# One hand-planned instruction list for four layers instead of three lists, and a new order of the first transfers

## The chip, the cores and the metric

One core of a Trainium2 chip runs the whole program. The metric is device time in microseconds of one execution, as the median of several runs. The engines are PE (TensorE, matrix products), DVE (VectorE), ACT (ScalarE), POOL (GpSimd) and SP (SyncE, which here issues every DMA). Each engine works through its own queue strictly in order; they meet at semaphores.

## The reference

Four layers run one after another on four images of 192 channels and 56 x 56 pixels, all in float32:

```
# layer 0: batch norm over the batch, 1x1 conv to q, k, v (6 heads of 32)
xn   = (x - mean) * rsqrt(var + eps) * gamma + beta        # mean, var over all four images
attn = softmax(conv7x7([q * scale, k]) + rel_bias)          # 49 logits per head and pixel
out  = sum over the 49 neighbours of attn * v               # then projection, residual
x    = x1 + c2(gelu(c1(x1)))                                # MLP of 768
# layer 1: a gate for each channel
filt = chosen per channel from 32 cosine bases, by a small network on image 0
y    = relu(bn1(w1d @ sum(pooled7x7(x) * filt)))            # one number per image and channel
x    = x * y + x
# layer 2: attention in overlapping 8x8 windows (stride 6), folded back by adding
out  = fold(exp(q k + bias - max) v) / fold(sum)            # projection, then gate by
out  = sigmoid(dwconv3(3x - pools of 2, 4, 8)) * out        # local high frequencies
x1   = x + out
x    = x1 + fc2(z1 * dwconv3(layer_norm(z2)))               # z1, z2 = gelu(fc1(norm(x1)))
# layer 3: selective scan in four directions
u    = silu(dwconv3(in_proj(norm(x)))); z = silu(...)
h_t  = exp(dt_t * A) * h_(t-1) + dt_t * B_t * u_t;  y_t = C_t h_t   # 4 states a channel
x    = x + out_proj(norm(sum of four directions) * z)
```

## The kernel before

**Staging.** `layers01` does layers 0 and 1, `layer2` and `layer3` the others. Between them whole images stand in DRAM (`x1`, `x2`). Channels lie on 96 partitions in two halves; pixels are cut into chunks of 448 (8 rows of an image, 7 chunks in each). Each of the three functions opens its own memory pools, loads its packed weights (`load_packs`, L219), clears and prepares its tiles, and closes its pools at the end, so the next function's tiles lie where the last one's were and can be written only when those are done.

**The order of the instructions.** Inside each function the work is written as many generators (threads), and a planner, the class `Order`, puts their steps into one list at build time. A step is yielded as an engine, a modelled cost, the buffers it takes and, for ACT, a table of functions. The planner keeps a model time for each engine. At every step it looks at the first 130 threads by their `place`, works out when each could start, and takes the one with the smallest start + 0.05 x place. Thus place is a soft priority in units of 0.05 us, and the queue of each of PE, ACT, DVE and POOL is this list, fixed at build time and run in order. There are three planners, one for each function, each beginning with model time zero and an empty list. The statements ahead of the planner's run (loads, clears, constants) are not in the list.

**The start.** `layers01` issues on SP: the three weight packs, 24 fills of `vmem` borders with zeros (L383, L385), then the four images (L391), each into a buffer from which DVE takes `bn_stats` (L394). The first image stays in `x`; the others share two buffers, so the fourth transfer waits until the statistics of the second are done. From the statistics come `bn_a`, `bn_c` (L402 to L404); PE multiplies them with weights (L421, L434); POOL clears `qk_in`, `xc` and `lg` (L482); then ACT copies the first pixels (L519) and PE makes values (L529, stored to `vmem` at L552) and the 7x7 convolution (L634).

**From layer 1 to layer 2.** DVE's `aggregate` steps (L789, L794, L803) end layer 0's attention. `mlp` then runs on PE and ACT for the last chunks (L869, L878, L884); `gate` (L1014 to L1042) forms one scale for each channel, loads each chunk back from `mid` (L1048), scales it on ACT (L1051, two instructions for each of 7 chunks) and stores it (L1053). Three buffers `xc` serve this. `layer2` then loads weights, multiplies weights with biases (L1111, L1124, L1136), clears 14 groups of tiles on POOL (L1158), and its first band `front(0)` loads rows (L1237), normalises them (L1193 to L1215), clears borders on POOL (L1242, L1251) and multiplies them to q and k (L1262).

**From layer 2 to layer 3.** Layer 2 is a chain of bands: `front`, `quad` (windows), `back`, then for each chunk `head`, `grow` and `tail` with two depthwise convolutions on DVE (nine taps each, L1341 and L1343) and products on PE up to L1506. After the last quad only heads, grows and tails are left. `layer3` loads weights, clears tiles on DVE and POOL (L1727, L1737, L1739) and starts with `begin(b, c)` for each chunk: a norm (L1768 to L1789), a product, and a depthwise convolution into `u`, for image 0 on DVE (L1855, L1857) and for the others on PE. From them come `prod` in DRAM, from which `load`, `sizes`, `decay` and `scan` run (L1989 to L2131); a scan group is one step of 448 pixels for half the channels, 56 groups for each image.

Of the kernel before, what the change touches and what calls it, by code (L numbers as in the profile page):

```python
# [20 lines left out]
HW = H * W  # L21
HALF = 96
# [218 lines left out]
class Order:  # L241
# [12 lines left out]
    def __init__(self, nc, **kinds):  # L254
        self.nc = nc
        self.engines = {}
        self.kinds = {k: [[0.0, t] for t in tiles] for k, tiles in kinds.items()}
        self.threads = []
        self.table = None
        self.end = 0.0  # L260

# [10 lines left out]
    def add(self, place, gen):  # L272
        self.threads.append([place, len(self.threads), gen, 0.0, next(gen)])

    def start(self, th):
# [10 lines left out]
        for kind in set(takes):  # L286
            n = takes.count(kind)
            free = sorted(s[0] for s in self.kinds[kind] if s[0] is not None)
            if len(free) < n:
                return None  # L290
            t = max(t, free[n - 1])
# [4 lines left out]
    def run(self):  # L296
        self.threads.sort(key=lambda th: th[:2])
        while self.threads:
# [7 lines left out]
            for th in over:  # L306
                self.threads.remove(th)
# [12 lines left out]
            if th[4] is None:  # L320
                self.threads.remove(th)
# [26 lines left out]

EXP_LN, GELU = "natural_log_exp_and_others", "gelu_and_others"
# [3 lines left out]
def layers01(tc, x_in, packs, aps, dst):  # L353
# [6 lines left out]
    with ExitStack() as ctx:  # L360
        const = ctx.enter_context(tc.tile_pool(name="a_const", bufs=1))
        dram = ctx.enter_context(tc.tile_pool(name="a_dram", bufs=1, space=DRAM))
        w = load_packs(nc, const, packs, aps)
        ident = const.tile([128, 128], F32, name="a_ident")
        make_identity(nc, ident)


        NG = HEADS // 2
        vmem = [dram.tile([NG, PADW, PADW, 64], F32, name=f"vmem{j}") for j in range(2)]
        x = const.tile([128, 2, HW], F32, name="x")  # L370
        nc.gpsimd.memset(x[HALF:], 0.0)
        mid = [dram.tile([C, HW], F32, name=f"mid{b}") for b in range(B)]


        bn_a = const.tile([HALF, 2], F32, name="bn_a")
        bn_c = const.tile([HALF, 2], F32, name="bn_c")
        with tc.tile_pool(name="a_stat", bufs=2) as sp:
            zero = sp.tile([PADW, 3 * 64], F32, name="zero", bufs=1)
            nc.vector.memset(zero, 0.0)
            for v in vmem:  # L380
                for g in range(NG):
                    for y in (0, PADW - 3):
                        nc.sync.dma_start(v[g][:, y : y + 3].rearrange("x y c -> x (y c)"), zero)  # L383
                    for y in (0, PADW - 3):
                        nc.sync.dma_start(  # L385
                            v[g][y : y + 3].rearrange("x y c -> y x c"), zero.rearrange("p (x c) -> p x c", c=64)
                        )
            stats = sp.tile([HALF, 2, B * NCHUNK, nc.vector.BN_STATS_DIM], F32, name="stats", bufs=1)
            for b in range(B):
                t = x[:HALF] if b == 0 else sp.tile([HALF, 2, HW], F32, name="xs")  # L390
                nc.sync.dma_start(t, pixels(x_in[b]))  # L391
                for h in range(2):
                    for c in range(NCHUNK):
                        nc.vector.bn_stats(stats[:, h, b * NCHUNK + c, :], t[:, h, c * CH : (c + 1) * CH])  # L394
            mv = sp.tile([HALF, 2, 2], F32, name="mv", bufs=1)
            for h in range(2):
                nc.vector.bn_aggr(mv[:, h, :], stats[:, h].rearrange("p a b -> p (a b)"))
            std = sp.tile([HALF, 2], F32, name="std", bufs=1)
            nc.vector.tensor_scalar_add(std, mv[:, :, 1], EPS)
            nc.scalar.activation(std, std, AF.Sqrt)  # L400
            nc.vector.reciprocal(std, std)
            nc.vector.tensor_mul(bn_a, w["a96.bn_gamma"], std)  # L402
            nc.vector.tensor_mul(bn_c, mv[:, :, 0], bn_a)
            nc.vector.tensor_sub(bn_c, w["a96.bn_beta"], bn_c)  # L404


        qk_scale = const.tile([128, 1], F32, name="qk_scale")
        nc.vector.memset(qk_scale, 1.0)
        for r in range(2):
            nc.vector.memset(qk_scale[64 * r : 64 * r + 32, :], HD**-0.5)  # L410
        qk_bias = const.tile([128, HEADS], F32, name="qk_bias")
        v_bias = const.tile([112, C], F32, name="v_bias")
        rel_bias = const.tile([128, HEADS], F32, name="rel_bias")
        nc.sync.dma_start(v_bias, aps["vb"].to_broadcast([112, C]))
        nc.vector.tensor_scalar_add(rel_bias, w["a128.rel"], w["a128.dm_b"])
        with tc.tile_pool(name="a_ps0", bufs=1, space=PSUM) as ps0, tc.tile_pool(name="a_sb0", bufs=1) as sb0:
            pq = ps0.tile([128, HEADS], F32, name="pq")
            for r in range(2):
                for hd in range(HEADS):
# [1779 lines left out]
```

## Time and profile before

| what | value |
|---|---|
| median of 3 runs | 6847.67 us (6843.52 to 6848.31) |
| profiled execution, its own time | 6850.6 us |
| its span | 6848.8 us |
| DVE busy | 5982.6 us, 87%, 7513 instructions |
| PE busy | 5770.1 us, 84%, 43558 instructions |
| ACT busy | 2621.1 us, 38%, 4063 instructions |
| POOL busy | 1409.3 us, 21%, 1401 instructions |
| layers 0 and 1 | about 0 to 2992 us |
| layer 2 | about 2992 to 4909 us |
| layer 3 | about 4909 to 6849 us |

Times inside the program are counted from the span's start. An engine's share over the whole span is a mean over stages with different limits, so the views to read are those of single stretches: where both busy engines are low together, no engine sets the pace but a chain of waits. The chain view follows the work that ended last backwards, and shows in order of time what each piece was and how long it took. A tile's name stands left of the arrow, its sources right of it.

### The profile page before, as it was taken

How to read it: one execution, taken by the hardware profiler on the slowest of the kernel's cores; microseconds unless marked ns; L12 is line 12 of the kernel's file. 1: busy time of each engine (PE TensorE's matmuls, PEld its weight loads, DVE VectorE, ACT ScalarE, POOL GpSimd, SP SyncE). 2: the span in 40 equal slices, each digit the busy share in tenths (PEclk: the TensorE clock that was granted, in tenths of full speed). 3: DMA queues.
4: the chain of work that ended last, by engine and by line, in shares of the span. 5: the costliest groups of instructions: out<-in, count | busy, mean ns of one | idle time of the engine just before them, and what ended most of it. 6: DMA issues, size and time to landing. Idle time of an engine off the chain costs nothing.

```text
span 6848.8 us, 107270 instructions
## 1 busy us (share of the span) xinstructions
PE 5770.1 (84%) x43558; PEld 2650.3 (39%) x43558; DVE 5982.6 (87%) x7513; ACT 2621.1 (38%) x4063; POOL 1409.3 (21%) x1401
## 2 busy tenths in 40 slices
PE   4999979999999996768888788886579889889777
PEld 2445434444444442335444444453223223222211
DVE  2799999999999999828999899898687887887997
ACT  1111112222222111125555455454266666666544
POOL 0000000000000000022122322220114544544564
PEclk9999989999999998879999899997799999999998
DMA  3222112221222113120000000000035565655654
GB/s 95 57 53 64 36 29 57 55 66 36 51 62 66 36 38 80 45 58 16 18 16 17 17 19 15 19 18 9 24 99 131 145 157 128 161 135 137 170 150 117
DMA packets 252042, 462.65 MB, mean 68 GB/s; under 512 B 30388, under 2 KB 237964, under 8 KB 240412
## 3 DMA queue, kind: packets, MB, share of 16 engines
q1 hardware_dynamic: 251548, 455.80, 26.4%
q8 instruction: 343, 5.62, 0.4%
q14 instruction: 151, 1.24, 0.1%
HBM read 238.58 MB, written 62.96 MB: 44 GB/s over the span
## 4 chain that ended last, share of the span: by engine, by line
DVE 49%; PE 35%; issue 7%; ACT 5%; DMA 2%; POOL 2%; SPq 0%; DVEq 0%; POOLq 0%; ACTq 0%
DVE pr L789 9%; DVE oa L794 7%; PE a_bank L634 6%; DVE bg L1343 5%; DVE ob L794 4%; PE c_bank L1864 4%; DVE st L2103 3%; DVE bxn L1343 3%; PE c_bank L1821 2%; PE a_bank L869 2%; PE a_bank L884 2%; PE c_bank L2081 2%; PE c_bank L2126 2%; DVE c_bank L2087 2%; PE bank L1506 1%
## 5 line engine op out<-in xcount | busy, mean ns | idle before, releaser
L789 DVE TENSOR_TENSOR pr<-vdx,attn 112x1792 f32<-112x1792 f32 (+4 forms) x720 | 1185.6, 1648 | 19.0
L634 PE MATMUL a_bank<-qk_in,w_a 64*49 64x392 f32 x9408 | 1161.2, 497 | 0.0
L2110 POOL TENSOR_TENSOR da<-st,bc 128x448 f32<-128x448 f32 x672 | 856.6, 1280 | 840.1 <-DVE st L2103 632.1
L794 DVE TENSOR_TENSOR oa<-oa,pr 112x1792 f32<-112x1792 f32 (+1 forms) x423 | 764.9, 1808 | 0.0
L634 PE MATMUL a_bank<-qk_in,wd 64*49 64x392 f32 x4032 | 694.6, 496 | 0.0
L2103 DVE TENSOR_TENSOR_SCAN st<-da,st,c_bank 128x448 f32<-128x448 f32 x576 | 647.2, 1133 | 0.7 <-ACT da L2056 0.7
masks.py:197 POOL MEMSET b_ident<- 128x128 f32 x1 | 0.2, 205 | 2857.5 <-DVE sc L1042 2857.5
L634 PEld LDWEIGHTS a_bank<-qk_in,w_a 64*49 64x49 f32 x9408 | 432.4, 120 | 397.7 <-issue 392.9
L2087 DVE TENSOR_TENSOR c_bank<-c_bank,bc 128x448 f32<-128x448 f32 x672 | 382.6, 617 | 113.1 <-PE c_bank L2081 112.6
L315 ACT ACT_TABLE_LOAD x372 | 477.3, 1283 | 6.5
L2056 ACT ACTIVATE da<-da,a_neg 128x448 f32<-128x448 f32 x672 | 413.8, 658 | 114.7 <-DMA da<-dt 112.8
L1343 DVE SCALAR_TENSOR_TENSOR bg<-bzpad,w_b,bg 128x448 f32<-128x448 f32 (+2 forms) x672 | 424.1, 687 | 0.0
L2126 PE MATMUL c_bank<-da,w_c 128*32 128x448 f32 x1344 | 352.2, 570 | 72.1 <-POOL da L2110 65.5
L794 DVE TENSOR_TENSOR ob<-ob,pr 112x1792 f32<-112x1792 f32 (+3 forms) x282 | 393.1, 1394 | 0.0
L878 ACT ACTIVATE hm<-a_bank,w_a 128x448 f32<-128x448 f32 x168 | 106.2, 633 | 641.7 <-PE a_bank L869 619.3
L869 PE MATMUL a_bank<-xc,w_a 128*128 128x448 f32 x672 | 297.4, 572 | 64.1 <-DVE xc L854 64.1
L2081 PE MATMUL c_bank<-du,w_c 32*128 32x448 f32 x1344 | 260.6, 624 | 105.8 <-DVE du L2071 62.9
L634 PEld LDWEIGHTS a_bank<-qk_in,wd 64*49 64x49 f32 x4032 | 249.2, 120 | 256.6 <-issue 254.7
L1432 PE MATMUL bank<-bxn,w_b 128*128 128x448 f32 (+2 forms) x672 | 293.6, 566 | 23.7 <-DVE bxn L1215 17.8
L586 ACT ACTIVATE qk_in<-a_bank,qk_bias,qk_scale 64x224 f32<-64x224 f32 (+5 forms) x288 | 146.1, 525 | 420.8 <-PE a_bank L571 418.5
L884 PE MATMUL a_bank<-hm,w_a 128*96 128x448 f32 x672 | 288.5, 561 | 21.1 <-ACT hm L878 21.0
L1864 PE MATMUL c_bank<-pad,diag 128*96 128x448 f32 (+2 forms) x756 | 297.4, 543 | 2.3 <-ACT pad L1832 2.3
(307 smaller groups left out, 9937.9 us busy)
## 6 DMA issues: line engine op xcount, KB each, us to landing
da<-dt SPq DMA_DIRECT2D x672, 224.0 KB
vdx<-vmem SPq DMA_DIRECT2D x168, 476.0 KB
bc<-prod SPq DMA_DIRECT2D x224, 224.0 KB
row<-x SPq DMA_DIRECT2D x56, 336.0 KB
x<-x SPq DMA_DIRECT2D x4, 2352.0 KB
vmem<-vt SPq DMA_DIRECT2D x56, 168.0 KB
xc<-x SPq DMA_DIRECT2D x56, 168.0 KB
mid<-xc SPq DMA_DIRECT2D x56, 168.0 KB
```

The lines of the kernel that those rows point to most:

```text
L315: self.nc.scalar.preload_act_table_set(table)
L634: nc.tensor.matmul(py[a][outs[g], : 7 * W].rearrange("p (y x) -> p y x", x=W), wt[halves[a], dx], q[halves[a], r, i0 + m : i0 + m + 7, dx ...
L789: nc.vector.tensor_mul(pr, vv, wt)
L794: nc.vector.tensor_add(og, og, before)
L869: nc.tensor.matmul(ph[:, :CH], w["a128.c1T"][:, k, 128 * m : 128 * m + 128], xt[:, k], start=(k == 0), stop=(k == 1),)
L884: nc.tensor.matmul(acc[h][:HALF, :CH], w["a128.c2T"][:, m, HALF * h : HALF * h + HALF], hm, start=(m == 0), stop=(m == 5),)
L1343: nc.vector.scalar_tensor_tensor(dst, x, wt[:, t : t + 1], dst, ALU.mult, ALU.add)
L1864: nc.tensor.matmul(rows2(pc[:HALF, : n * W]), diag[:, h, t], pad[:, h, at + t // 3 : at + t // 3 + n, t % 3 : t % 3 + W], start=(t == 0), ...
L2087: nc.vector.tensor_mul(tiles[j][:, :SCH], tiles[j][:, :SCH], b_)
L2103: nc.vector.tensor_tensor_scan(sts[j][:, r], da[:, r], tiles[j][:, :SCH][:, r], first, ALU.mult, ALU.add)
L2110: nc.gpsimd.tensor_mul(da, sts[j], c_)
L2126: nc.tensor.matmul(py[32 * j : 32 * j + 32, :SCH], w["c128.sum"], das[j], start=True, stop=True)
```

## The change

1. **One list.** There is one `Order` for all functions. Threads can be added while it runs (`add` with a layer's name, sorted in by place), kinds of buffers can be given later (`give`), and it counts the open threads of each layer. `layer2` and `layer3` become generators that are themselves threads of the list, at places 84 and 240. Their loads, clears and constants become steps. Layer 2's threads get 150 added to their places, layer 3's 330.
2. **Memory from two sides.** What layer 0's attention alone uses (`x`, `qk_in`, `vdx`, `pr`, `attn` and others) lies on the right side, the rest of layers 0 and 1 on the left. When the last sums are done, the right side is closed and layer 2's weights and most of its tiles are put there and cleared. When all threads of layers 0 and 1 have been placed, their left side is closed and layer 2's tiles for windows are put there; `bxn` is now cleared on DVE. When all quads and bands are placed, that left side goes to layer 3's weights, rows and `u` of image 0, and its threads join the list; `begin` of image b asks that layer 2's tails of that image are placed. When layer 2 has no open thread, `y`, the second `u` and the buffers of the scans take the right side.
3. **The start.** The images are issued first, then the weights, `v_bias`, and the zero fills.
4. **The last image's gate.** For image 3 the scaling runs on POOL as `tensor_scalar_mul`; the other images stay on ACT.

The diff without its changes of indentation, cut:

```diff
 class Order:
...
+    def give(self, **kinds):
+        for k, tiles in kinds.items():
+            self.kinds[k] = [[self.end, t] for t in tiles]
...
-    def add(self, place, gen):
-        self.threads.append([place, len(self.threads), gen, 0.0, next(gen)])
+    def add(self, place, gen, layer):
+        self.open[layer] += 1
+        bisect.insort(self.threads, [place, next(self.count), gen, self.end, next(gen), layer])
+
+    def drop(self, th):
+        self.threads.remove(th)
+        self.open[th[5]] -= 1
...
+BASE2, BASE3 = 150, 330
...
-def layers01(tc, x_in, packs, aps, dst):
+def layers01(tc, pools, x_in, packs, aps, dst):
...
+    ctx, early, dram, banks = pools["01"], pools["01 sums"], pools["dram"], pools["banks"]
+    att = early.enter_context(tc.tile_pool(name="a_att", bufs=1, side="right"))
-        w = load_packs(nc, const, packs, aps)
...
-        x = const.tile([128, 2, HW], F32, name="x")
+    x = att.tile([128, 2, HW], F32, name="x")
...
+        stats = sp.tile([HALF, 2, B * NCHUNK, nc.vector.BN_STATS_DIM], F32, name="stats", bufs=1)
+        for b in range(B):
+            t = x[:HALF] if b == 0 else sp.tile([HALF, 2, HW], F32, name="xs")
+            nc.sync.dma_start(t, pixels(x_in[b]))
...
+        w = load_packs(nc, const, packs, aps)
+        nc.sync.dma_start(v_bias, aps["vb"].to_broadcast([112, C]))
             for v in vmem:
                 for g in range(NG):
...
-            stats = sp.tile([HALF, 2, B * NCHUNK, nc.vector.BN_STATS_DIM], F32, name="stats", bufs=1)
...
+        if u == NG * B - 1:
+            order.marks.add("sums of 01")
...
-                yield on_act(CH, CH, ready=order.end + 3)
                 for h in range(2):
+                if b < B - 1:
+                    yield on_act(CH, ready=None if h else order.end + 3)
                     nc.scalar.activation(xt[:HALF, h], xt[:HALF, h], AF.Copy, scale=sc[:, h : h + 1])
+                else:
+                    yield on_pool(CH, each=0.0015)
+                    nc.gpsimd.tensor_scalar_mul(xt[:HALF, h], xt[:HALF, h], sc[:, h : h + 1])
...
-def layer2(tc, src, packs, aps, dst):
+def layer2(tc, order, pools, src, packs, aps, dst):
...
+    yield lambda: "sums of 01" in order.marks
+    pools["01 sums"].close()
+    const = ctx.enter_context(tc.tile_pool(name="b_const", bufs=1, side="right"))
+    yield on_sp()
     w = load_packs(nc, const, packs, aps)
+    there = order.end + 12
...
+    for t in (*xl, *sq, *xn2s, p, apad, *zpads):
+        yield on_pool(1500)
+        nc.gpsimd.memset(t, 0.0)
...
+    yield on_pe(8 * 80, "bank", ready=there)
...
+    yield lambda: order.open["01"] == 0
+    pools["01"].close()
...
+    for i in range(2):
+        yield on_dve(1700)
+        nc.vector.memset(xns[i], 0.0)
+        for t in (qs[i], ks[i]):
+            yield on_pool(1600, each=0.0009)
+            nc.gpsimd.memset(t, 0.0)
+    for t in accs:
+        yield on_pool(3400, each=0.0009)
+        nc.gpsimd.memset(t, 0.0)
+    order.give(xl=xl, sq=sq)
...
-def layer3(tc, src, packs, aps, dst):
+def layer3(tc, order, pools, src, packs, aps, dst):
...
+    yield lambda: "2" in order.marks and order.at2["quad"] == 100 and order.at2["back"] == 20
+    pools["2 quads"].close()
+    const = pools["3"].enter_context(tc.tile_pool(name="c_const", bufs=1))
+    yield on_sp()
     w = load_packs(nc, const, packs, aps)
+    there = order.end + 8
...
+    for t in (*rows, *sqs, *pads):
+        yield on_dve(900)
+        nc.vector.memset(t[HALF:], 0.0)
+    yield on_pool(6000)
+    nc.gpsimd.memset(us[0][HALF:], 0.0)
...
         def begin(b, c):
...
+        yield lambda: order.at2["tail"] >= NCHUNK * (b + 1)
...
+    yield lambda: order.open["2"] == 0
+    pools["2"].close()
+    late = pools["3"].enter_context(tc.tile_pool(name="c_late", bufs=1, side="right"))
...
+    us += [late.tile([128, 2, HW], F32, name="u1")]
+    y = late.tile([128, 2, HW], F32, name="y")
...
-            layers01(tc, [x[b] for b in range(B)], packs[0], aps[0], x1)
-            layer2(tc, x1, packs[1], aps[1], x2)
-            layer3(tc, x2, packs[2], aps[2], [out[b] for b in range(B)])
+            order = layers01(tc, pools, [x[b] for b in range(B)], packs[0], aps[0], x1)
+            order.add(84, layer2(tc, order, pools, x1, packs[1], aps[1], x2), "later")
+            order.add(240, layer3(tc, order, pools, x2, packs[2], aps[2], [out[b] for b in range(B)]), "later")
+            with tc.manual_schedule(engines=engines):
+                order.run()
```

## The prediction

> **What bounds the kernel now.** I read the page first, then the busy times of stretches around the three places that the change touches, then the chain of waits there. The page gives the span, the busy time of each engine, and the busy tenths of 40 slices of 171.2 us each.
>
> ```profile
> span 6848.8 us, 107270 instructions
> ...
> PE   4999979999999996768888788886579889889777
> ...
> DVE  2799999999999999828999899898687887887997
> ...
> PEclk9999989999999998879999899997799999999998
> ```
>
> Inside the layers DVE or PE stands at 9 or near it; both are low together in slice 1 (start), slice 18 (2911 to 3082 us, layer 1 ends, layer 2 begins: PE 6, DVE 2) and slice 29 (4794 to 4965, layer 2 ends, layer 3 begins: 5 and 6). DVE is busy 5982.6 us of 6848.8, so 866 us hold all of its idle time. The next view gives busy time of each engine in the stretches of those places (columns: length, then busy time and count of PE, PEld, DVE, ACT, POOL, then clock, DMA share, GB/s).
>
> ```profile
> 0.00:94.00 94.00, 0.00 (x0) 0.00 (x0) 38.30 (x82) 1.89 (x4) 6.03 (x7) 1.00 0.60 154
> ...
> 2966.00:3025.60 59.60, 14.35 (x52) 10.08 (x52) 5.34 (x16) 10.76 (x18) 33.48 (x24) 0.50 0.39 116
> 4790.00:4909.00 119.00, 70.44 (x136) 29.51 (x136) 80.96 (x129) 33.35 (x40) 3.72 (x7) 0.73 0.03 8
> 4909.00:4999.00 90.00, 52.33 (x118) 20.31 (x119) 60.63 (x82) 32.35 (x43) 22.48 (x19) 0.77 0.20 57
> ```
>
> PE does nothing for 94 us; no engine but POOL is half busy in the second stretch; DVE is idle 38 us of the third and 29 of the fourth. The chain of waits (start, length, what) names what ends each hole:
>
> ```profile
> 38.63 23.77 DMA xs<-x
> 62.42 7.48 DVE stats L394 x14
> 69.92 14.11 DMA xs<-x
> ...
> 2989.16 2.77 DMA x<-xc
> 2992.15 3.02 POOL bxn L1158 x2
> ...
> 3024.94 0.63 POOL bxn L1251
> 3025.61 7.54 PE bank L1262 x16
> ...
> 4900.04 8.40 PE bank L1506 x24
> 4909.41 2.20 DMA w_c<-c
> 4911.66 10.59 POOL u L1727 x2
> ```
>
> At the start the images are last in SP's queue, behind 24 zero fills. At 2992 POOL clears layer 2's memory, which waited for layer 1's last store. At 4909 layer 3 starts from nothing.
>
> **Part 1, the start.** SP issues the first image at 37.30 now, and would at 0.75, where its first transfer stands today: 36.5 us earlier for the images and the statistics, which depend on nothing else. The fourth image still waits for a buffer (69.92 today, 33.4 then) and lands at 84.03 - 36.5 = 47.5. The weights are queued behind it; today their 3540 KB land 10.6 us after the last issue (1.66 to 12.27), so they land near 58, and `bn_a` (93.77 - 36.5 = 57.3) needs them: I take 1 us lost; 10 if they share badly with the image. Small DVE steps on weights, hidden today in the wait (6.3 us before 20 us), now follow: 1.3 us. The two `qk_in` clears (100.90 to 104.6, after L434 today) lie in memory from the right that nothing held before, so they move into the wait: 3.8 us gained, 0 if they still wait. The 24 zero fills move behind the weights; 18 of them took 14.4 to 37.3 = 22.9 us once the weights were through, so they end near 82, and the first store of `vt` (111.21 today, due at 72) is 10 us late. Behind it in SP's queue stand only more of these stores. `vt` has one buffer, so DVE's next add waits and two of eight banks stay full; PE's third pair of value matmuls comes at 129.5 - 38 = 91, so PE's convolution work covers it. Without that cover it costs 10. Sum: 36.5 - 1 - 1.3 + 3.8 = **38 us** (26 to 41). PE is 20 of 20 us busy from 120 on, so this shift stays.
>
> **Part 2, layer 1 to layer 2.** From 2892 (last `ob` step) to 2958 the chain is the MLP of image 3 on PE and ACT, DVE idle 60 of 73 us, POOL all of it. Into this cover go layer 2's weights (2051 KB), its clears of `bxl`, `bsq`, `bxn2`, `bp`, `bapad`, `bzpad` (2.69 + 2.65 + 1.81 + 5.32 + 1.16 + 3.61 = 17.2 us of POOL) and the products of weights and biases. The 44 small matmuls took 2.69 + 1.44 + 5.28 = 9.4 us at clock 0.50; in the last chunk PE waits 0.78 us six times for `hm`. At full clock L421's 48 took 4.88 us, so 44 cost 4.5, less some gaps: 3 us lost (0 to 9).
>
> The last image's 14 scalings go to POOL. No row shows that operation there. From below: a clear of 128x448 takes 0.57 us; from above: a product of two 128x448 tiles takes 1.28. The nearest are copies of 128x256, 0.36 with DVE idle and 0.73 with DVE busy. DVE is idle here, so I take 0.7 for 448; ACT needs 8.3 us for the 14, POOL 9.8: 1.5 lost (0 to 9.6). The Trainium skill ("GPSIMD Engine Reference", 4.1 Engine selection) would keep elementwise work off GpSimd, and its 3.1 gives 1.8 cycles at 1.2 GHz per element at best: an estimate of 0.67 us each, 9.4 us in all, with which the term would be 1.1; no trace here shows it.
>
> In return the second batch of `mid` loads is freed sooner: today its stores (2966.76) wait 9.04 us behind the weights' transfer, against 2.8 for the later ones (2980.68, 2989.16): 6.2 gained. After the last scaling only the `bq`, `bk`, `bacc` clears (3.03 + 3.03 + 5.92) and the four first-band clears (1.76) stand before L1262: 13.7 us. Today from the last store's landing at 2992 to 3025.6 it is 33.5: 19.8 gained. `bxn` goes to DVE, idle. The load and norm of the first band (3007.9 to 3019.7, 11.8 us) run beside POOL and fit. Sum: 19.8 + 6.2 - 3 - 1.5 = 21.5, and 1.5 for the landing if the left memory that POOL clears first did not hold `xc`: **23 us** (10 to 32).
>
> **Part 3, layer 2 to layer 3.** When the 100 quads and 20 bands are through (the last use of their memory is L1316, about 4763), layer 3's weights, constants and clears go in, some 25 us of steps one after another, so its first chunks can start about 4790. Layer 2's end leaves DVE 38 us there; the eight gaps of 1.9 us or more sum to 32.7, and each loses about 0.8 to a tap already running: 26 us usable. A chunk of image 0 costs DVE 2 x (0.5 + 5.75) + 2 x 1.08 = 14.7, so 1.8 chunks fit. The price is a later drain: eight times 0.65 us, and table switches, since layer 3 needs others than layer 2. I take 8 us (0 to 20). The ACT table load rows are 1.28 us each and the next instruction starts 0.02 us later; at two switches for each of 1.8 chunks that is 4.6 us of ACT, which is busy 33 of 119. The Trainium skill ("ScalarE: Activation LUTs", Table sets: the hidden batching unit) says to batch by table set, which interleaving breaks, and counts 2.66 us a switch with a drain that these rows do not have; by it these four would cost 10 us, with which the drain would lose about 11 and the total be 3 smaller.
>
> Today the third chunk's convolution ends at 4992.4, 83.4 us after the drain; the first scans need that chunk. Then 1.2 chunks remain at 17.6 us each (4974.8 to 4992.4): 21 us. Gain 83.4 - 8 - 21 = **54 us**; with 0 chunks done, a cold chain of 12 us and 20 us of delay, none; with three done and no delay, 83. The clears of `y` and `u1` (5.32 each) lie on POOL, which waits for the first scan anyway (to 5034 today).
>
> **Sum.** 38 + 23 + 54 = 115 us against the profiled execution's own 6850.6 (span 6848.8 and 1.8 around it): 6735.6. That execution is 2.9 above the median of 6847.7, so the median goes to **6733**.
>
> **Rivals.** (a) The drain takes in only the set-up, because the planner's handicap (0.05 us for each unit of place, about 278 against 250: 1.4 us) and DVE leave no room for chunks: part 3 is 20, total 38 + 23 + 20 = 81, **6767**. For it: DVE 20 of 20 us in several slices there; against: the eight gaps. (b) More fits, as PE's clock of 0.73 rises when it has more to do (four matmuls L1193 took 3.30 us at 4728, six took 2.42 at 4751): parts 2 and 3 give 30 and 78, **6702**. Only some steps of the drain are PE's. (c) Slower: the queues of layers 2 and 3 are drawn anew, since one greedy list starts them from other engine times, and the scans fall worse. 224 scan groups (L2071 to L2131) run at 7.86 us each (440 us for 56); from 0.51 us more per group the 115 are gone; at 0.8 more it is 6733 + 179 = **6912**. For it: POOL waits 569.9 us for DVE's scans there, so order matters; against: a constant on every place changes no choice inside a layer, and three images begun from different states took 440 us with DVE busy 357, 364 and 363. (d) The added chunks do not start at all, if something of image 0 is still asked for; then part 3 is only the set-up, as (a); no condition in the code does that, `tail` of image 0 was over long before.
>
> **How the numbers follow.** The forecast 0.62, (a) with (d) 0.20, (b) 0.12, (c) 0.06. The range: all upper terms give 41 + 32 + 83 = 156, **6692**; all lower ones at once 26 + 10 + 0 = 36, 6812, which needs three misses together; I end at 28 + 10 + 15 = 53, **6795**, which takes in (a). About 0.2% (14 us) is what a measurement tells from no change: faster 0.92, within 0.03 (small terms and some of (c)), slower 0.05.
>
> **What would show it.** First PE work at 58 instead of 94; L1262's first matmul about 61 us (38 + 23) before 3025.6; POOL's scalings near 0.7 us; some 1.8 chunks of L1855/L1857 on DVE before layer 2's last L1506; first L2103 115 us earlier than 5033; 440 us for each image after. The forecast is wrong if the images after that take another time, or the drain from the last quad to the last L1506 grows by more than 20 us.

## The result, and the profile after

The changed kernel takes 6757.66 us (median, 6752.91 to 6759.15), the kernel before in the same rounds 6847.99 (6843.52 to 6855.57): a ratio of 0.9869, interval 0.9854 to 0.9883. The profiled execution's span fell from 6848.8 to 6754.8 us, by 94.0. The forecast was 115 us. The page after, with the rows that answer to those of the prediction:

```profile
span 6754.8 us, 107251 instructions
...
PE   6999889999999995768888788786689889889776
...
DVE  2999999999999999838999899898888887887997
...
PEclk9999889999999997889999899998799999999998
```

PE's first slice went from 4 to 6. The dips where layers meet are still there, in the same slices: PE 6 and DVE 3 in the 18th, PE 6 and DVE 8 in the 28th and 29th, where DVE had 6 in the 29th before. The busy times of the stretches, in the same columns (length, then busy time and count of PE, PEld, DVE, ACT, POOL, then clock, DMA share, GB/s):

```profile
0.00:57.00 57.00, 0.00 (x0) 0.00 (x0) 32.72 (x72) 1.66 (x3) 10.69 (x10) 1.00 0.93 237
2928.20:2974.00 45.80, 4.49 (x8) 1.52 (x6) 4.73 (x5) 3.00 (x4) 32.83 (x24) 0.50 0.31 88
4746.00:4868.50 122.50, 84.59 (x184) 36.08 (x184) 101.90 (x161) 45.06 (x57) 5.43 (x11) 0.81 0.06 17
4868.50:4935.30 66.80, 48.60 (x110) 17.24 (x111) 52.91 (x79) 41.30 (x57) 12.11 (x8) 0.87 0.38 100
```

PE waits 57 us at the start instead of 94. Between the last image's gate and layer 2's first quads (second row) POOL still works 33 of 46 us. The drain of layer 2, its end after the last quads (third row), has DVE busy 102 us of 122.5 where it was 81 of 119, and what follows it is 67 us long to the first scan.

How the 94.0 us came together, by one event after another in the two profiles:

| stretch, ending with | before at | after at | gained | forecast |
|---|---|---|---|---|
| start: first convolution on PE, L634 / L656 | 119.97 | 79.58 | 40.4 | 38 |
| layers 0 and 1: last sums, L803 / L825 | 2892.24 | 2848.86 | 3.0 | 0 |
| layer 1 to 2: first L1262 / L1318 | 3025.61 | 2974.03 | 8.2 | 23 |
| layer 2: last step before the drain, L1215 / L1271 | 4763.10 | 4709.16 | 2.4 | 0 |
| layer 2 to 3: first scan, L2103 / L2160 | 5033.23 | 4935.32 | 44.0 | 54 |
| layer 3: end of the span | 6848.8 | 6754.8 | -3.9 | 0 |

Rows of 3 us are not to be read closely: in the twelve profiles of the changed kernel and its variants, the last sums lie between 2848.8 and 2857.1, though the first convolution on PE differs by 1.4 us at most. Two of them have the same PE instructions in the same order there, yet one is granted a clock of 0.98 between 200 and 300 us and the other 0.91, and it ends the layers 6.4 us later. So events of one stretch are counted from the last event of the stretch before.

### The profile page after: what moved, and what is told of

Read it like the earlier page. It is cut to its first block, busy times and chain, and to the rows that moved or that the text cites. A ratio compares the mean times of both kernels' runs of the same rounds, so it can differ in the third digit from the quotient of the medians.

```text
span 6754.8 us, 107251 instructions
## 1 busy us (share of the span) xinstructions
PE 5757.1 (85%) x43558; PEld 2642.5 (39%) x43558; DVE 5976.0 (88%) x7515; ACT 2615.2 (39%) x4049; POOL 1414.7 (21%) x1413
## 4 chain that ended last, share of the span: by engine, by line
DVE 26%; PE 20%; issue 4%; ACT 4%; POOL 1%; DMA 1%; SPq 0%; DVEq 0%; POOLq 0%; ACTq 0%
DVE bg L1399 6%; PE bank L1921 4%; DVE st L2160 3%; DVE bxn L1399 3%; PE bank L1878 2%; DVE bank L2144 2%; PE bank L2138 2%; PE bank L2183 2%; PE bank L1562 1%; PE bank L1265 1%; DVE bacc L1711 1%; PE bank L2011 1%; PE bank L1249 1%; DVE e L1650 1%; PE bank L1488 1%
## 5 line engine op out<-in xcount | busy, mean ns | idle before, releaser
L656 PE MATMUL bank<-qk_in,w_a 64*49 64x392 f32 x9408 | 1157.4, 496 | 0.0
L656 PE MATMUL bank<-qk_in,wd 64*49 64x392 f32 x4032 | 691.3, 494 | 0.0
L2160 DVE TENSOR_TENSOR_SCAN st<-da,st,bank 128x448 f32<-128x448 f32 x576 | 646.8, 1132 | 0.7 <-ACT da L2113 0.7
L656 PEld LDWEIGHTS bank<-qk_in,w_a 64*49 64x49 f32 x9408 | 431.7, 120 | 396.1 <-issue 390.4
L2144 DVE TENSOR_TENSOR bank<-bank,bc 128x448 f32<-128x448 f32 x672 | 382.7, 617 | 114.6 <-PE bank L2138 114.1
L1399 DVE SCALAR_TENSOR_TENSOR bg<-bzpad,w_b,bg 128x448 f32<-128x448 f32 (+2 forms) x672 | 423.6, 685 | 0.0
L2183 PE MATMUL bank<-da,w_c 128*32 128x448 f32 x1344 | 355.5, 575 | 72.7 <-POOL da L2167 66.9
L2138 PE MATMUL bank<-du,w_c 32*128 32x448 f32 x1344 | 261.6, 626 | 105.0 <-DVE du L2128 62.8
L656 PEld LDWEIGHTS bank<-qk_in,wd 64*49 64x49 f32 x4032 | 247.8, 119 | 256.7 <-issue 254.8
L893 PE MATMUL bank<-xc,w_a 128*128 128x448 f32 x672 | 296.8, 571 | 58.6 <-DVE xc L878 58.6
L908 PE MATMUL bank<-hm,w_a 128*96 128x448 f32 x672 | 288.5, 561 | 20.2 <-ACT hm L902 20.2
L1921 PE MATMUL bank<-pad,diag 128*96 128x448 f32 (+2 forms) x756 | 297.4, 543 | 2.3 <-ACT pad L1889 2.3
```

Of the source, the lines that this page charges most:

```text
L656: nc.tensor.matmul(py[a][outs[g], : 7 * W].rearrange("p (y x) -> p y x", x=W), wt[halves[a], dx], q[halves[a], r, i0 + m : i0 + m + 7, dx ...
L1399: nc.vector.scalar_tensor_tensor(dst, x, wt[:, t : t + 1], dst, ALU.mult, ALU.add)
L1921: nc.tensor.matmul(rows2(pc[:HALF, : n * W]), diag[:, h, t], pad[:, h, at + t // 3 : at + t // 3 + n, t % 3 : t % 3 + W], start=(t == 0), ...
L2138: nc.tensor.matmul(tiles[j][:, :SCH], w["c96.rep"][r], du[r], start=True, stop=True)
L2144: nc.vector.tensor_mul(tiles[j][:, :SCH], tiles[j][:, :SCH], b_)
L2160: nc.vector.tensor_tensor_scan(sts[j][:, r], da[:, r], tiles[j][:, :SCH][:, r], first, ALU.mult, ALU.add)
```

## The experiments

Line numbers are those of the changed kernel; in an edited one they can differ by up to six, as the quoted rows show.

**The start alone.** In the kernel before, the four images are transferred first, then weights, bias and zero fills; nothing else.

```diff
-            w = load_packs(nc, const, packs, aps)
...
+            for b in range(B):
+                t = x[:HALF] if b == 0 else sp.tile([HALF, 2, HW], F32, name="xs")
+                nc.sync.dma_start(t, pixels(x_in[b]))
...
+            w = load_packs(nc, const, packs, aps)
+            nc.sync.dma_start(v_bias, aps["vb"].to_broadcast([112, C]))
```

> The kernel before with one part of the change alone: the four images are transferred first, then the weights, the value bias and the zero fills; the three lists and the memory plan stay. Theory (the start is a part by itself): the images land 37 us earlier, the qk_in clears stay behind the products on DVE and cost the 3.8 us that the whole change saved there, so the last sums of layer 1 come at about 2892.2 - 38 = 2854 and the time is about 6848 - 38 = 6810, 36 to 40 below before. Rival 1 (the transfers that were moved back - weights, bias, zeros - end last and hold the products or the first columns): less than 25 us, a time over 6823. Rival 2 (the gain is taken back where layers 2 and 3 are planned): the last sums are 38 us earlier but the time is not.

Measured: 6805.2 us (6804.57 to 6820.27), ratio 0.9934 (0.9916 to 0.9952); first PE convolution at 83.0 instead of 120.0, 36.9 earlier, and the last sums at 2858.0, 34.2 earlier (38 expected). The theory holds at the place where it acts; rivals 1 and 2 fall. With the two-sided memory the same event comes at 79.6: the `qk_in` clears that move into the wait (on POOL at 6.64 us instead of 63.89) are worth 3.5. The time itself fell by 45.7, outside the 36 to 40 expected; the interval (33 to 58 us) doesn't tell it from 37, and the rest stays unexplained: in the profiles 34.2 of the 45.8 us are there at the last sums, and 2.0, 4.0 and 5.5 come in the gate, layer 2 and layer 3, whose instructions are the same. Single profiles thus differ by some 5 us in layer 3 alone, which is more than the 3.9 lost there in the table above.

**Who scales the last image.** First all images on ACT, then the last image on POOL with a constant in place of the column:

```diff
-                if b < B - 1:
-                    yield on_act(CH, ready=None if h else order.end + 3)
-                    nc.scalar.activation(xt[:HALF, h], xt[:HALF, h], AF.Copy, scale=sc[:, h : h + 1])
-                else:
-                    yield on_pool(CH, each=0.0015)
-                    nc.gpsimd.tensor_scalar_mul(xt[:HALF, h], xt[:HALF, h], sc[:, h : h + 1])
+                yield on_act(CH, ready=None if h else order.end + 3)
+                nc.scalar.activation(xt[:HALF, h], xt[:HALF, h], AF.Copy, scale=sc[:, h : h + 1])
```

```diff
-                    nc.gpsimd.tensor_scalar_mul(xt[:HALF, h], xt[:HALF, h], sc[:, h : h + 1])
+                    nc.gpsimd.tensor_scalar_mul(xt[:HALF, h], xt[:HALF, h], 0.5)
```

> The changed kernel with the last image's 14 scalings back on ACT. In the changed kernel they took 1.38 us each on POOL (8.30 us for six), on ACT before 0.58 to 0.60. Theory (they are on the chain from the gate to the first L1318): 14 x 0.8 = 11 us less between the gate and the last store, first L1318 at about 2963 instead of 2974, time about 6746 to 6749 against 6757.7. Rival (POOL's next work and the landings hide it): first L1318 within 3 us of 2974 and the time within 3 us of 6757.7.

> The changed kernel with the last image scaled on POOL by the constant 0.5 instead of by its gate, so the computation leaves the last image's gate out; all else as it was. It measures the price of a scaling on POOL: 1.38 us with the gate's column as the factor, where my prediction took 0.7. Theory A (the element rate of POOL on 96x448 f32 costs it): 1.3 to 1.4 us each here too. Theory B (reading the factor from a column costs it): 0.6 to 0.8 us each.

The rows of the scalings (start, length, engine, line, what; in brackets the idle time before and what ended it), first the changed kernel's POOL:

```profile
2928.57 8.30 POOL L1080 TENSOR_SCALAR xc<-xc,sc 96x448 f32<-96x448 f32 x6 [61.51 <-DVE sc L1066]
2941.98 8.30 POOL L1080 TENSOR_SCALAR xc<-xc,sc 96x448 f32<-96x448 f32 x6 [5.10 <-DMA xc<-mid]
2954.65 2.78 POOL L1080 TENSOR_SCALAR xc<-xc,sc 96x448 f32<-96x448 f32 x2 [4.38 <-DMA xc<-mid]
2960.47 1.54 POOL L1231 MEMSET bq<- 96x1736 f32 x1 [3.04 <-issue]
```

then ACT in the kernel before (second and third batch), ACT in the version with ACT, POOL with the constant, and DVE in the last experiment below:

```profile
2979.43 3.61 ACT L1051 ACTIVATE xc<-xc,sc 96x448 f32<-96x448 f32 x6 [10.46 <-DMA xc<-mid]
2987.91 1.23 ACT L1051 ACTIVATE xc<-xc,sc 96x448 f32<-96x448 f32 x2 [4.88 <-DMA xc<-mid]
```

```profile
2934.86 3.46 ACT L1076 ACTIVATE xc<-xc,sc 96x448 f32<-96x448 f32 x6 [8.54 <-DVE sc L1066]
```

```profile
2926.51 7.79 POOL L1080 TENSOR_SCALAR xc<-xc 96x448 f32<-96x448 f32 x6 [27.54 <-DMA xc<-mid]
```

```profile
2922.51 2.26 DVE L1080 TENSOR_SCALAR xc<-xc,sc 96x448 f32<-96x448 f32 x6
```

For six scalings POOL took 8.30 us (1.38 each), ACT 3.46 (0.58), DVE 2.26 (0.38). With a constant POOL still took 1.30 each, so the column costs only 0.08, as theory A has it; how much of the rest goes by the element and how much is fixed for each instruction, one tile size does not tell. (One run, 6754.8 us.) With ACT the first quads come 35.6 us after the gate's scale (L1066) instead of 45.8, which is 10.1 of the 11 expected. In the seven profiles with POOL's scalings by the column and covered clears that distance is 45.6 to 45.8. The time was 6751.72 us (6748.87 to 6755.87), ratio 0.9851 (0.9836 to 0.9866). That agrees with the theory, but the interval overlaps with the changed kernel's, and in this profile layers 0 and 1 alone were 6.4 us slower; the position is what decides.

**When layer 2's products of weights and biases run.**

```diff
+    yield lambda: order.open["01"] == 0
     yield on_pe(8 * 80, "bank", ready=there)
```

> The changed kernel with layer 2's weight-by-bias products (L1164 to L1191, 44 small matmuls, and the steps that use them) placed only after the last piece of layers 0 and 1, where before had them. Counted from the last sums (L825), because that point itself differs by up to 6 us between profiles of the same instructions. Theory (the products and the lower clock that follows them, 0.73 and 0.59 in two stretches of 5 us, hold the gate back): the gate's scale (L1066) is ready about 73 us after the last sums instead of 79.4, the products hide beside POOL's 13.5 us of clears behind the last store, and the first L1318 comes about 119 us after the last sums instead of 125.2; time some 6 us under the changed kernel's, about 6751. Rival 1 (the products are then late for L1318): the gate's scale is earlier but the first L1318 is not. Rival 2 (the gate is late for another reason than the products): the scale stays at 79.

The scale came 73.1 us after the last sums instead of 79.4, the first quads 118.8 instead of 125.2: as the theory has it. Time 6750.11 us (6745.66 to 6754.7), ratio 0.9851 (0.9834 to 0.9868). PE's rows (as above) show why the cost was more than the products' own time. Changed kernel, then products late:

```profile
2887.81 2.75 PE L1191 MATMUL bank<-w_b,w_b 96*128 96x1 f32 x24
2890.42 5.37 PE L870 MATMUL bank<-ot,w_a 128*96 128x448 f32 x8
2895.72 3.35 PE L893 MATMUL bank<-xc,w_a 128*128 128x448 f32 x4
```

```profile
2895.47 3.68 PE L870 MATMUL bank<-ot,w_a 128*96 128x448 f32 x8
2899.08 1.86 PE L893 MATMUL bank<-xc,w_a 128*128 128x448 f32 x4
```

The same eight matmuls take 5.37 us behind the products and 3.68 without them. The clock of these stretches in the changed kernel (the third number from the end):

```profile
2885.00:2890.00 5.00, 5.00 (x37) 3.70 (x34) 3.23 (x7) 1.60 (x3) 0.00 (x0) 1.00 0.19 54
2890.00:2895.00 5.00, 5.00 (x14) 1.67 (x13) 1.59 (x5) 0.00 (x0) 0.00 (x0) 0.73 0.30 84
2895.00:2900.00 5.00, 4.22 (x7) 1.32 (x6) 1.89 (x5) 0.63 (x1) 0.00 (x0) 0.59 0.00 0
```

This does not happen each time. Eight profiles have the products inside the MLP; in six the clock falls behind them and the scale comes at 79.4 to 80.6, in two (the chunks-held and the constant-factor runs) it stays at 1.00, the eight matmuls take 3.73 and the scale comes at 74.3 and 74.2. In the four profiles of the changed kernel's kind without products there, they take 3.68 and the clock stays at 1.00. So the products cost 1.2 us and the clock behind them, when it falls, 5 to 6 more.

**The bacc clears later.**

```diff
-    for t in accs:
-        yield on_pool(3400, each=0.0009)
-        nc.gpsimd.memset(t, 0.0)
...
-        add(5 * j - 3, zero(j)) if j >= 2 else None
+        add(5 * j - 3, zero(j))
```

> The changed kernel with the two bacc clears (2.99 us each on POOL, the last before the first L1318) moved to the places where each is first added to. Theory (POOL's clears set the first L1318): POOL is done 6 us earlier, and the next in the row is the first layer norm and POOL's four small border clears behind it, which end 2 to 4 us earlier, so the first L1318 comes 2 to 4 us earlier than 125.2 us after the last sums; time some 3 us under the changed kernel's. Rival (the layer norm chain sets it already): no change. Rival 2 (the clears are late for the first quads): L1318 earlier, but the time is not.

Nothing moved: first quads 125.0 us after the last sums, 6760.38 us (6752.5 to 6772.19), ratio 0.9867 (0.9848 to 0.9887). The rows say why. The planned order put the same work back into the same place on POOL, ahead of the border clears that the quads wait for:

```profile
2967.20 5.92 POOL L1337 MEMSET bacc<- 128x3472 f32 x2
2973.07 0.38 POOL L1295 MEMSET bxn<- 128x336 f32 x1
```

So the run doesn't test the theory. What it would be worth stays open: the layer norm's last DVE step (2970.27, 0.85 long) bounds it at about 2 us, since the first border clear could start at 2971.1 and not at 2973.1.

**Layer 2's clears without their cover.**

```diff
+    yield lambda: order.open["01"] == 0
     for t in (*xl, *sq, *xn2s, p, apad, *zpads):
```

> The changed kernel with the clears and the weight-by-bias products of layer 2's set-up placed only after the last piece of layers 0 and 1 (its weights are still transferred early). This takes the cover of image 3's MLP away from 17.2 us of POOL's clears. Theory (POOL's clears behind the last store set the first L1318, and taking 19.8 us of them out was the gain of this stretch; the products cost 6.3 of it): the gate's scale about 73 us after the last sums instead of 79.4, the first L1318 about 139 us after them instead of 125.2, time about 13 us over the changed kernel's, 6768 to 6774. Rival (the weights' early transfer was the gain, POOL's clears were not): first L1318 at 119 after the last sums as when only the products were late, time 6750.

The first quads came 133.9 us after the last sums, neither the theory's 139 nor the rival's 119. Time 6764.14 us (6760.69 to 6771.57), ratio 0.9866 (0.9845 to 0.9887). POOL behind the last scaling:

```profile
2949.57 2.78 POOL L1080 TENSOR_SCALAR xc<-xc,sc 96x448 f32<-96x448 f32 x2 [4.33 <-DMA xc<-mid]
2952.30 2.69 POOL L1148 MEMSET bxl<- 128x1008 f32 x3
...
2970.08 1.54 POOL L1232 MEMSET bq<- 96x1736 f32 x1 [0.29 <-issue]
```

These clears lie in memory that no transfer held, so POOL runs them during the last store's landing, for which it otherwise waits 3.04 us. From the end of the last scaling to the first quads it is 31.3 us (2952.35 to 2983.63), with the cover 16.6. The cover is worth 14.7, about what the 17.2 us of clears and 0.8 of a constant's steps come to, less the 3.0 of the landing. In the kernel before the same distance was 36.5 (2989.14 to 3025.61). POOL's rows account for these other 5.2 us without the weights: 3.0 of waiting for the landing (to 2992.15) and 3.0 of two `bxn` clears, which stand on DVE now, less the 0.8 of the constant. Scale at 73.1 again, with the products late.

**Layer 3's chunks, and its set-up, held back.** First the chunks alone, then also the clears, constants and weight steps in front of them (the weights' transfer stays in the drain in both):

```diff
-        yield lambda: order.at2["tail"] >= NCHUNK * (b + 1)
+        yield lambda: order.open["2"] == 0
```

> The changed kernel, but the chunks of layer 3's first image may begin only once all of layer 2 is placed; the clears and weights stay where they are. Theory (chunks in the drain are worth 17.6 us each, less what they cost the drain): the 1.5 chunks that ran in the drain come after it, +26 us, and the drain is about 5 us shorter (13.5 less the 8.4 of the clears), so first L2160 at about 4935.3 + 21 = 4956 and time about 6779. Rival (the set-up alone gave the gain of this stretch, what my prediction named as its case a): time within 5 us of 6757.7.

```diff
+    yield lambda: order.open["2"] == 0
     for t in (*rows, *sqs, *pads):
```

> The changed kernel with layer 3's clears, constants and weight steps, and so its chunks, placed only after all of layer 2 (its weights are still transferred in the drain). Beside the run in which only the chunks were held back (6791.2; first L2160 at 4968.0, 101 us after the end of the drain), it tells what the set-up alone was worth. Theory (set-up 20 us, as my case a had it; chunks the rest): the drain is 6 us shorter without the clears on DVE, the first L2160 comes about 121 us after its end, at about 4982, and the time is 6800 to 6810. Rival (the chunks alone are the gain, the set-up fits beside the first chunks): first L2160 within 3 us of 4968, time about 6791.

No chunks in the drain: 6791.18 us (6785.56 to 6793.34), ratio 0.9907 (0.9892 to 0.9922). No set-up either: 6793.48 (6786.09 to 6799.39), ratio 0.9908 (0.989 to 0.9926). Each profile splits at the end of the drain (the last L1570):

| kernel | drain, from L1271 | then to the first scan | both |
|---|---|---|---|
| before | 145.9 | 124.3 | 270.1 |
| set-up and chunks held back | 145.0 | 115.6 | 260.6 |
| chunks held back | 153.3 | 103.5 | 256.8 |
| changed | 159.4 | 66.8 | 226.2 |
| clears on POOL (next) | 155.6 | 66.4 | 222.0 |

In the seven profiles with neither the drain nor its set-up edited, the drain is 158.3 to 159.4 us long and what follows it 66.6 to 66.9, so differences of over 2 us in this table are clear of that spread. Chunks in the drain save 36.7 us behind it and cost 6.1 in it: 30.6 net, where 21 was expected. The set-up steps save 12.1 behind it and cost 8.3 in it: 3.8 net, so the number of the rival came true, though its reason (that the set-up fits beside the first chunks) didn't: it is paid for in the drain. The remaining 9.5 came though both were held back. The weights are there, and POOL, which before cleared two `u` tiles on the chain from 4911.66 to 4922.24, clears the first before the drain ends:

```profile
4848.62 5.32 POOL L1776 MEMSET u<- 32x6272 f32 x1
```

DVE's first add of layer 3 (L1770, here L1826) then starts 13.7 us after the drain instead of 24.1; how much of that is the weights' and how much the clear's, these runs do not tell.

The busy times of the drain and of what follows it (columns as above), changed kernel, then chunks held back:

```profile
4709.16:4868.54 159.38, 93.07 (x211) 40.75 (x209) 137.34 (x238) 53.28 (x68) 12.43 (x20) 0.75 0.08 23
4868.54:4935.30 66.76, 48.60 (x110) 17.24 (x111) 52.88 (x78) 41.26 (x57) 12.11 (x8) 0.87 0.38 100
```

```profile
4711.20:4864.50 153.30, 70.29 (x161) 30.89 (x160) 115.68 (x205) 41.52 (x51) 10.18 (x14) 0.72 0.05 17
4864.50:4968.00 103.50, 71.58 (x161) 25.51 (x160) 73.78 (x110) 54.26 (x74) 13.67 (x14) 0.87 0.28 75
```

DVE's convolution of layer 3's chunks in the changed kernel (L1912 and L1914, nine steps for each half of a chunk) begins in the drain:

```profile
4789.33 0.67 DVE L1912 TENSOR_SCALAR u<-pad,w_c 96x392 f32<-96x392 f32 x1
...
4863.16 3.54 DVE L1914 SCALAR_TENSOR_TENSOR u<-pad,w_c,u 96x448 f32<-96x448 f32 x5
...
4868.99 5.70 DVE L1914 SCALAR_TENSOR_TENSOR u<-pad,w_c,u 96x448 f32<-96x448 f32 x8
...
4889.01 5.70 DVE L1914 SCALAR_TENSOR_TENSOR u<-pad,w_c,u 96x448 f32<-96x448 f32 x8
```

The second row ends the first half of chunk 1, the third its second half just after the drain's end, the fourth the third chunk. 21.7 us of DVE work went into the drain, for 6.1 us more of its length; behind it 20.9 us of DVE work is gone, and the 15.8 us of waits that stood between its steps.

**Layer 3's eight clears on POOL instead of DVE.**

```diff
     for t in (*rows, *sqs, *pads):
-        yield on_dve(900)
-        nc.vector.memset(t[HALF:], 0.0)
+        yield on_pool(900, each=0.0009)
+        nc.gpsimd.memset(t[HALF:], 0.0)
```

> The changed kernel with the eight clears of layer 3's row, sq and pad tiles on POOL instead of DVE. In the changed kernel they took 8.4 us of DVE at 4711 to 4719, in front of the drain's first hx step. Theory (that is why the drain ended 13.5 us late and not 8): first hx step 5 to 8 us earlier, last L1570 at 4861 to 4864 instead of 4868.5, first L2160 at 4928 to 4931 instead of 4935.3, time 6750 to 6753. Rival (the drain is late through the early chunks' own taps on DVE and table loads on ACT): last L1570 within 2 us of 4868.5, time unchanged. A second rival (POOL now clears in front of the chunks' own POOL steps): the chunks come later, time above 6757.7.

The changed kernel's DVE between L1271 and the first step of the drain that sets its length (L1427):

```profile
4709.16 1.55 DVE L1271 TENSOR_TENSOR bzpad<-bzpad,bank 128x1344 f32<-128x1344 f32 x1 [7.94 <-ACT bank L1269]
4710.96 3.63 DVE L1773 MEMSET row<- 32x896 f32 x4 [0.24 <-issue]
...
4719.15 0.69 DVE L1427 TENSOR_TENSOR hx<-bp 96x224 f32<-96x224 f32 x2
...
4720.13 1.35 DVE L1397 TENSOR_SCALAR bg<-bzpad,w_b 128x448 f32<-128x448 f32 x3
```

and with the clears on POOL:

```profile
4713.90 0.68 DVE L1427 TENSOR_TENSOR hx<-bp 96x224 f32<-96x224 f32 x2
...
4714.89 3.29 DVE L1397 TENSOR_SCALAR bg<-bzpad,w_b 128x448 f32<-128x448 f32 x3
```

L1427 follows L1271 after 1.5 us instead of 10.0, and the drain is 3.8 shorter, the first scan 4.2 earlier: half of the 8.5. L1397 took 3.29 us where it took 1.35; the rest was lost in later steps that I did not follow one by one. The time doesn't tell this: 6759.67 us (6752.47 to 6764.13), ratio 0.9864 (0.9846 to 0.9883).

**The repairs together**, with the last image on ACT and then on DVE, and the changed kernel again beside the second:

> Four repairs of the changed kernel together: the last image's scalings on ACT, the row, sq and pad clears on POOL, the weight-by-bias products after the last piece of layers 0 and 1, the bacc clears later. From the earlier runs and the positions in the traces: 10 for the scalings (45.8 to 35.6 us from the gate's scale to the first L1318), 6 for the products, 2 to 4 for the bacc clears, 4 for the row, sq and pad clears. Theory (they add up, since each is on the one path through these two stretches): about 22 us, a time of 6731 to 6738 against 6757.7. Rival (they hide each other: once the gate is earlier, the landing of the last store or the layer norm decides): 10 to 14 us, 6744 to 6748.

> The changed kernel itself once more, unedited, on the chip and in the rounds of the next run, so that the two can be set side by side. Expected 6750 to 6762, and positions within 3 us of its first profile when they are counted from the last sums: gate's scale 79.4, first L1318 125.2, first L2160 2086.

> The four repairs together, but with the last image's 14 scalings on DVE instead of ACT. DVE did two products by a column on 96x448 f32 in 0.93 us, 0.46 each, ACT 0.58. Theory (the engine's own time for the six scalings of a batch is on the chain): 3 batches of 6, 6 and 2 give about 1.6 us, so 33.5 us from the gate's scale to the first quads' L1312 of this kernel, against 35.1 with ACT; the time 20 to 25 us under the changed kernel's of the same rounds, not to be told from the version with ACT (6734.5). Rival (the last image's pieces now stand behind weight steps of layer 2 on DVE): 36 us or more.

| kernel | us | ratio to before | scale after the last sums | first quads after the scale |
|---|---|---|---|---|
| changed | 6757.66 | 0.9869 (0.9854 to 0.9883) | 79.4 | 45.8 |
| repairs, ACT | 6734.52 (6721.9 to 6749.74) | 0.9827 (0.9806 to 0.9848) | 71.1 | 35.1 |
| changed, again | 6761.46 (6754.42 to 6769.82) | 0.9881 (0.9868 to 0.9895) | 80.6 | 45.8 |
| repairs, DVE | 6733.91 (6728.88 to 6744.49) | 0.9844 (0.983 to 0.9857) | 73.1 | 33.6 |

The repairs add up, as far as they act; the `bacc` clears stand in their old place here too. Alone the other three gave 10.1, 6.3 and 4.2, 20.6 in all; together the first scan comes 22.3 us (ACT) and 22.0 us (DVE) earlier after the last sums than in the changed kernel (its first profile for ACT, its second for DVE), and by the medians the second is 27.5 us faster than the changed kernel in the same rounds. ACT or DVE makes 1.5 us at the place, and no difference that the time shows. Both are faster than the kernel before and the changed one.

## Why the prediction held, point by point

The time lies inside the range and on the forecast's side, 24.7 us above the forecast.

**Part 1 (38).** Right: 40.4 at the first convolution. The statistics are done 37.1 us earlier and not 34.2, since the weights had landed by 55.9, before `bn_a` asked for them; the two terms of 1 and 1.3 us were not lost. The `qk_in` clears gave 3.5 of 3.8. As forecast, the store of `vt` made DVE wait (13.1 us for its buffer) and PE did not wait for that.

**Part 2 (23).** The mechanisms were right, two prices too small; measured 8.2. From the last store's issue to the first quads 19.9 was gained (forecast 19.8): 17.2 by the clears under cover, the rest by `bxn`'s on DVE. The waits for the second and third batch fell from 15.3 to 9.5 us, 5.9 less (6.2). But the term "1.5 lost (0 to 9.6)" for the scalings was 11.1, 19.4 us on POOL against ACT's 8.3. A scaling took 1.38 us, above my upper bound of 1.28, a product of two tiles with more partitions: that row was no bound. The term "3 us lost (0 to 9)" for the products was 6.3, and 1.2 where the clock stayed at 1.00; the lower clock behind them was not in the sum. The 1.5 for the landing failed: POOL waits 3.04 us. Its row names no releaser, but the same wait, 3.17 us, is ended by the store's landing in the version with the constant. 19.9 + 5.9 - 11.1 - 6.3 = 8.4.

The Trainium skill ("GPSIMD Engine Reference", 4.1 Engine selection) would keep elementwise work off GpSimd, and here the rows agree: 1.38 us against 0.58 on ACT and 0.38 on DVE. The same row of the page calls work with one input roughly line-rate; here POOL took more than three times as long as DVE. The 1.8 cycles an element that its section 3.1 gives as the best case, an estimate of 0.67 us, were not reached even with a constant factor (1.30).

**Part 3 (54).** Measured 44.0. Chunks do start in the drain and are most of the gain, but "a later drain, I take 8" was 13.5, and 26.2 us were left behind it to the third chunk's convolution, not 21: chunk 0 and half of chunk 1 were convolved by then, 1.5 and not 1.8. What my working left out: the steps of the set-up run on the same DVE on which the drain depends. The eight clears alone hold it for 8.5 us; I had counted them among "25 us of steps" without a place. 83.4 - 13.5 - 26.2 = 43.7.

**The rivals.** (a) gave 6767 for a drain that takes in only the set-up; the time is near that number by chance. The chunks ran, and without them it is 6791: the set-up was worth 13.3 (9.5 + 3.8), not 20. (b) needed a faster clock in parts 2 and 3; it rose in the drain (0.73 to 0.81 in the third row) but the gains were smaller, not larger. (c) did not happen: from the first scan to the end it is 1819.5 us against 1815.6, 0.02 us more for each of the 224 groups, against 0.51 that would have decided. (d) is refuted with (a).

## What to carry to other kernels

A step that moves into the shadow of another is free only if its engine is free there: ask for each moved instruction which engine it needs and who waits for that engine next, and small clears were the ones forgotten here. For an operation that no row shows, a row of another operation is no bound, so a price on which many instructions hang is better measured, or kept off the path. Look at the sum of both sides of a border: steps moved from behind the drain into it saved 12.1 us and cost 8.3.

## What was not expected of the hardware

- POOL took 1.30 us for a product of 96x448 f32 with a constant and 1.38 with a column, ACT 0.58, DVE 0.38.
- The granted clock fell to between 0.50 and 0.90 in stretches of 5 us just behind 40 matmuls of one column, with PE busy 5.00 of 5 us in the first of them, in six of eight profiles. The runs do not show why it stayed at 1.00 in the other two.
- DVE's products by a column are held up by POOL's clears. Two on 96x384 took 0.73 us with POOL idle (chunks held back) and 4.73 in the run with layer 3's set-up held back, where a clear of 5.32 us ran beside them; three on 128x448 (L1397) took 1.35 and 3.29. The fused multiply-adds (L1399) took 1.87 with POOL idle and 1.86 beside a clear. In all 14 profiles, 34 of the 840 products of L1397 (L1341 in the kernel before) into `bg` on 448 pixels began while a POOL clear of more than 1.2 us had at least 0.6 us to run: these took 1.36 us or more each, the other 806 took 0.96 or less. 336 multiply-adds into `bg` began like this, and none took over 0.90. The rows, chunks held back, set-up held back, and clears on POOL:

```profile
4732.68 0.73 DVE L1803 TENSOR_SCALAR w_c<-w_c,w_c 96x384 f32<-96x384 f32 x2
```

```profile
4864.80 5.32 POOL L2244 MEMSET u<- 32x6272 f32 x1
...
4865.93 4.73 DVE L1804 TENSOR_SCALAR w_c<-w_c,w_c 96x384 f32<-96x384 f32 x2
```

```profile
4715.18 2.75 POOL L1773 MEMSET pad<- 32x1276 f32 x2
...
4717.88 5.56 POOL L1775 MEMSET u<- 32x6272 f32 x1
...
4718.56 1.86 DVE L1399 SCALAR_TENSOR_TENSOR bg<-bzpad,w_b,bg 128x448 f32<-128x448 f32 x3
```

The Trainium skill ("GPSIMD Engine Reference", 1. Specifications) names POOL's SBUF interfaces as shared with VectorE, with contention for DVE instructions in a two-port mode or with two inputs in SBUF. The products agree with it if they ran in such a mode, which no run here shows; the multiply-adds, which read two tiles in SBUF, were not held up by these clears.
